# The end of an attention kernel: divisors through a permutation product, the residual in PSUM, projections moved into the last block, and a norm spread over more periods

## The chip, the cores and the metric

The kernel runs on one core of a Trainium2 chip. The time is the device time of one launch in microseconds (us), the median of several runs. Engines are named as the profile names them: PE is TensorE (matmul), DVE VectorE, ACT ScalarE, POOL GpSimd, and SP the queue that issues all DMAs here. Instructions of one engine start in the order in which the program lists them.

## What is computed

Two layers run on x of shape (2, 2048, 512) with a condition vector per batch row. The first is a state-space block: norm, a linear recurrence, a residual, and a feed-forward part. The second is attention with 16 heads of 32 features. Cut to what the change touches, the second layer ends so:

```python
energy = jnp.einsum('bhqd,bhkd->bhqk', q, k)
att = jax.nn.softmax(energy, axis=-1) / D ** 0.5
out = jnp.einsum('bhqk,bhkd->bhqd', att, v)
out = jnp.moveaxis(out, 1, 2).reshape(B, N, D)
out = out @ Wp.T + bp
h1 = out + hidden
h2 = _sln(h1, w, ln_g, ln_b, Wg, bg, Wb, bb)
return h2 + h1
```

`_sln` is a norm over the 512 features with a gain and a shift that come from the condition. `hidden` is the output of the first layer.

## The kernel before

**First layer, to about 1390 us.** Chunks of 512 rows pass through norm, recurrence and feed-forward; the norm is `ln_stats` with `rsqrt` (L116), four columns at a time: a first guess by integer arithmetic and three Newton steps of four VectorE instructions each. `rsqrt` is called 24 times here, and once at the very end of the kernel.

**Attention, from about 1450 us.** A block is one batch row, one pair of heads and 512 queries; there are 64, listed in `blocks`, and the last of batch 1 are ordered so that the queries 1536 to 2047 of the last two pairs come at the end. A block takes eight periods. In a period TensorE makes scores: two maxima probes `m` (`across`, L773), one or two score tiles that are kept (`keep`, L762), sometimes a score tile that is made again (`make`, L816), and the products of probabilities with values for two key tiles of the period before (`weighted`, L828). VectorE reads `m` (`top`, L785), keeps a running maximum (`run`, L771) and shifts the fresh scores (`pT`, L820); GpSimd shifts the kept ones (`take_off`, L812); ScalarE copies kept scores (L766) and takes exponentials (L825). Score tiles `s` have two PSUM buffers, `m` has one. The block runs ahead: maxima of a block are gathered 15 periods before they are used, and the shift of a block goes through DRAM and back into a tile of 128x1024 (`spread`, L799).

Values carry 32 columns of ones, so that the output `o` of a pair, one PSUM tile, holds the outputs of two heads in partitions 0 to 31 and 96 to 127 and their divisors, each repeated 32 times, in partitions 32 to 63 and 64 to 95. After the last key tile `weighted` copies `o` to `raw` (L842) and writes divisors to `sd` and outputs to `od` in DRAM.

**The order of everything else** is written out by hand. `after(j, what, ...)` puts work at the start of period j, `closing(j, what, ...)` after that period's second exponential. Entries of one period run in the order in which they were entered. In the text offset means the period within a block, 0 to 7.

When all heads of 512 queries are there, `fetch_sums`, `invert` (reciprocal, L875) and a write bring 1/divisor to `invd`. Each tile of 128 queries is then fetched (`fetch`, L878: six DMAs), divided on GpSimd (`divide`), projected (`project`: four matmuls), and normalised: `moments` (residual add, statistics), `deviation` (ten small VectorE instructions: 1/sqrt by three Newton steps), `last_norm` on ScalarE, and `add_t` and `close` on GpSimd, then the output DMA. For batch 0 the 16 tiles go beside the attention of batch 1, two tiles in each three blocks: projection in offsets 6, 7, 0 and 1, `moments` at the close of offset 1, `deviation` at the close of offset 2, `last_norm` and `add_t` in offset 5, `close` in offset 7. For batch 1 all steps of a tile are packed more densely.

**The last 512 queries of batch 1** have their own functions. `end_fetch` (L972) loads outputs, divisors and residual rows of the first twelve heads in one period before the last block, 19 DMAs; `end_fetch_more` loads the outputs of heads 12 and 13; `end_divide` divides on GpSimd. After the last block `end_project` (L1000) projects three groups of four heads, and `end_last` (L1010) sends the divisors of heads 12 to 15 through DRAM, inverts them, divides, projects the fourth group, adds the residual, and normalises and writes four tiles.

The lines that set the order of the end before:

```python
after(NP * (N - 1) + 3, end_fetch_more)
for g in range(NG - 1):
    after(j + 5 + g, end_divide, g)
after(NP * N + 2, end_project, list(range(NG - 1)))
after(NP * N + 20, end_last)
```

with j two periods ahead of the last block, whose first period is `NP * (N - 1)`.

Of the kernel before, what the change touches and what calls it, by code (L numbers as in the profile page):

```python
# [8 lines left out]
F32 = mybir.dt.float32  # L9
# [3 lines left out]
I32 = mybir.dt.int32  # L13
# [6 lines left out]
P = 128  # L20
# [19 lines left out]
def tile_s5_block_then_sln_attention(  # L40
# [75 lines left out]
    def rsqrt(v, y, n):  # L116

        nc.vector.tensor_scalar(
            y.bitcast(I32), v.bitcast(I32), -0.5, float(0x5F3759DF), ALU.mult, ALU.add
        )  # L120
        for _ in range(3):
            a = small.tile([P, n], F32, name="rs_a", tag=f"rs_a{n}")
            nc.vector.tensor_mul(a, y, y)
            b = small.tile([P, n], F32, name="rs_b", tag=f"rs_b{n}")
            nc.vector.tensor_mul(b, a, v)
            c = small.tile([P, n], F32, name="rs_c", tag=f"rs_c{n}")
            nc.vector.tensor_scalar(c, b, -0.5, 1.5, ALU.mult, ALU.add)
            nc.vector.tensor_mul(y, y, c)

    def ln_stats(src, n, mean, rstd):  # L130

# [696 lines left out]
    def weighted(n, kt, first, final):  # L828

        if first:  # L830
            outs[n] = ps_o.tile([P, CH], F32, name="o")
        x = probs.pop((n, kt))
        v = vst[pair_of[n] % 2]
        for e in range(2):
            nc.tensor.matmul(  # L835
                outs[n][64 * e : 64 * e + 64, :], v[:, kt, e : e + 2, :], x[:, e, :],
                start=first, stop=final,
            )
        if final:
            b, p, c = blocks[n]  # L840
            raw = work.tile([P, CH], F32, name="raw")
            nc.scalar.copy(raw, outs.pop(n))  # L842
            cols = slice(c * CH, (c + 1) * CH)
            for e in range(2):
                j = 2 * p + e
                nc.sync.dma_start(sd[b][j : j + 1, cols], raw[32 + 32 * e : 33 + 32 * e, :])
            for e in range(2):
                j = 2 * p + e
                if n == len(blocks) - 1:
                    dst = ends["o"][1][64 + HD * e : 64 + HD * e + HD, 1, :]  # L850
                else:
                    dst = od[b][HD * j : HD * j + HD, cols]
                nc.sync.dma_start(dst, raw[96 * e : 96 * e + 32, :])


    held, ending = {}, {}
# [51 lines left out]
            nc.tensor.matmul(py, o4[:, g, :], wp[:, g, :], start=g == 0, stop=g == NG - 1)  # L908
        held[b, qt] = o4, h, py

    def moments(b, qt):

        o4, h, py = held[b, qt]
        nc.vector.tensor_add(h, py, h)
        st = small.tile([P, 6], F32, name="st3")
        nc.vector.bn_stats(st, h)
        mv = small.tile([P, 2], F32, name="mv3", bufs=4)
        nc.vector.bn_aggr(mv, st)
        held[b, qt] = h, o4.rearrange("p g q -> p (g q)"), mv

    def add_t(b, qt):
        h, ht, *_ = held[b, qt]
        nc.gpsimd.tensor_tensor(ht, h, ending[b][1], ALU.add)

    def deviation(b, qt):

        h, ht, mv = held[b, qt]
        v = small.tile([P, 1], F32, name="v3")
        c = small.tile([P, 1], F32, name="c3")
        y = small.tile([P, 1], F32, name="scale3", bufs=3)  # L930
        shift = small.tile([P, 1], F32, name="shift3", bufs=3)
        nc.vector.tensor_scalar(v, mv[:, 1:2], EPS, None, ALU.add)
        nc.vector.tensor_scalar(
            y.bitcast(I32), v.bitcast(I32), -0.5, float(0x5F3759DF), ALU.mult, ALU.add
        )
        nc.vector.tensor_scalar(v, v, -0.5, None, ALU.mult)
        for _ in range(3):
            nc.vector.tensor_scalar(c, y, y, v, ALU.mult, ALU.mult)
            nc.vector.tensor_scalar(y, c, 1.5, y, ALU.add, ALU.mult)
        nc.vector.tensor_scalar(shift, mv[:, 0:1], -1.0, y, ALU.mult, ALU.mult)  # L940
        held[b, qt] = h, ht, y, shift

    def last_norm(b, qt):

# [19 lines left out]
        nc.sync.dma_start(out[b, qt * P : (qt + 1) * P, :], y)  # L964


    LB, LC = NB - 1, NQ - 1

    def spare(name):
# [2 lines left out]
    def end_fetch():  # L972
        cols = slice(LC * CH, (LC + 1) * CH)
        ends["o"] = [spare("o01"), spare("o23")]
        ends["by"] = [spare("by01"), spare("by23")]
        ends["h"] = [spare("h01"), spare("h23")]
        for g in range(NG - 1):
            nc.sync.dma_start(ends["o"][g // 2][:, g % 2, :], od[LB][g * P : g * P + P, cols])
            end_divisors(range(4 * g, 4 * g + 4))
        for t in range(TT):  # L980
            at = slice((LC * TT + t) * P, (LC * TT + t + 1) * P)
            nc.sync.dma_start(ends["h"][t // 2][:, t % 2, :], x2[LB][at, :])

    def end_fetch_more():
        cols = slice(LC * CH, (LC + 1) * CH)
# [7 lines left out]
                ends["by"][j // 8][at, j // 4 % 2, :], invd[LB][j : j + 1, cols].to_broadcast([HD, CH])  # L993
            )

    def end_divide(g):
        o, by = ends["o"][g // 2][:, g % 2, :], ends["by"][g // 2][:, g % 2, :]
        nc.gpsimd.tensor_tensor(o, o, by, ALU.mult)

    def end_project(groups):  # L1000
        if "py" not in ends:
            ends["py"] = [ps.tile([P, 2, CH], F32, name="py4", tag="s", bufs=2) for _ in range(2)]
        for t in range(TT):
            for g in groups:
                nc.tensor.matmul(
                    ends["py"][t // 2][:, t % 2, :], ends["o"][g // 2][:, g % 2, t * P : (t + 1) * P],
                    wp[:, g, :], start=g == 0, stop=g == NG - 1,
                )

    def end_last():  # L1010
        late = slice(NH - 4, NH)
        fetch_sums(LB, LC, late, 32)
        invert(LB, LC, late, 32)
        end_divisors(range(NH - 4, NH))
        o, by = ends["o"][1][:, 1, :], ends["by"][1][:, 1, :]
        nc.vector.tensor_tensor(o, o, by, ALU.mult)
        end_project([NG - 1])
        g_row, t_row = ending[LB]
        mv = small.tile([P, TT, 2], F32, name="mv4")
        for t in range(TT):  # L1020
            h, py = ends["h"][t // 2][:, t % 2, :], ends["py"][t // 2][:, t % 2, :]
            nc.vector.tensor_add(h, py, h)
            st = small.tile([P, 6], F32, name="st3")
            nc.vector.bn_stats(st, h)
            nc.vector.bn_aggr(mv[:, t, :], st)
        v = small.tile([P, TT], F32, name="v4")
        scale = small.tile([P, TT], F32, name="scale4")
        shift = small.tile([P, TT], F32, name="shift4")
        nc.vector.tensor_scalar(v, mv[:, :, 1], EPS, None, ALU.add)
        rsqrt(v, scale, TT)  # L1030
        nc.vector.scalar_tensor_tensor(shift, mv[:, :, 0], -1.0, scale, ALU.mult, ALU.mult)
        for t in range(TT):
            qt = LC * TT + t
            h = ends["h"][t // 2][:, t % 2, :]
            y = ends["o"][t // 2][:, t % 2, :]
            nc.scalar.activation(y, h, AF.Identity, bias=shift[:, t : t + 1], scale=scale[:, t : t + 1])
            nc.gpsimd.tensor_tensor(h, h, t_row, ALU.add)  # L1037
            nc.vector.tensor_tensor(y, y, g_row, ALU.mult)  # L1038
            nc.vector.tensor_tensor(y, y, h, ALU.add)  # L1039
            nc.sync.dma_start(out[LB, qt * P : (qt + 1) * P, :], y)  # L1040


# [44 lines left out]
    for b in range(NB):  # L1087
        for c in range(NQ):
            j = NP * (blocks.index((b, NPAIR - 1, c)) + 1) + 1
            if (b, c) == (LB, LC):  # L1090
                most = slice(0, NH - 4)
                j = NP * (N - 1) - 2
                after(j - 3, fetch_sums, b, c, most)
                after(j - 1, invert, b, c, most)
                after(j + 1, end_fetch)
                after(NP * (N - 1) + 3, end_fetch_more)
                for g in range(NG - 1):
                    after(j + 5 + g, end_divide, g)
                after(NP * N + 2, end_project, list(range(NG - 1)))
                after(NP * N + 20, end_last)  # L1100
                continue
            after(j, fetch_sums, b, c)
            after(j + 2, invert, b, c)
# [2 lines left out]
            for t in range(TT):  # L1106
                qt = c * TT + t
                if b == LB:
                    k = j + 3 + 2 * t
                    after(k + 3, project, b, qt)  # L1110
                    after(k + 3, moments, b, qt)
                else:

                    k = NP * (NPAIR * NQ * (b + 1) + 2 + 3 * qt // 2) + 3
                    for g in range(NG):
                        after(k + 3 + g, project, b, qt, (g,))
                    closing(k + 6, moments, b, qt)
                last = k + 3 if b == LB else k + 6
                after(k if b == LB else k - 2, fetch, b, qt)
                after(k + 2, divide, b, qt)  # L1120
                (after if b == LB else closing)(last + 1, deviation, b, qt)
                after(last + (2 if b == LB else 4), last_norm, b, qt)
                after(last + (3 if b == LB else 6), close, b, qt)
                if b != LB:
                    after(last + 4, add_t, b, qt)

    def run_due(j):
        for what, args in due.pop(j, ()):
# [117 lines left out]
```

## Time and profile before

| what | us |
|---|---|
| median of 3 runs | 3510.64 |
| lowest, highest | 3507.99, 3518.59 |
| the profiled execution | 3509.6 |
| its span in the profile | 3507.7 |

The profiled execution ran at a mean granted TensorE clock of 0.991. Busy time by stage, from the view that gives each engine's busy time in stretches (columns: stretch, length, then busy us of PE, its weight loads, DVE, ACT, POOL with the number of instructions, granted clock, DMA share, GB/s):

```profile
400.00:1300.00 900.00, 899.83 (x2316) 413.09 (x2315) 254.99 (x569) 136.04 (x197) 218.38 (x162) 1.00 0.12 42
...
1500.00:2000.00 500.00, 489.19 (x2093) 221.90 (x2093) 453.61 (x451) 444.10 (x484) 406.38 (x172) 1.00 0.28 67
...
2500.00:3000.00 500.00, 476.61 (x1941) 212.32 (x1941) 434.96 (x538) 403.57 (x440) 407.44 (x193) 1.00 0.33 79
...
3460.00:3508.00 48.00, 23.68 (x68) 8.07 (x68) 24.91 (x54) 9.74 (x12) 16.52 (x11) 0.83 0.12 42
```

In the first layer PE is busy all the time. In attention alone (1500 to 2000) PE has 97.8%, and VectorE, ScalarE and GpSimd have 81% to 91%. In the stretch in which batch 0 is normalised beside it (2500 to 3000) PE falls to 95.3%. In the last 48 us no engine is busy for more than half of the time.

### The profile page before, as it was taken

Reading aid. Unit: us, or ns where it says so; the run is one execution under the profiler, and the core shown is the slowest. Engines: PE = TensorE matmul, PEld = TensorE weight load, DVE = VectorE, ACT = ScalarE, POOL = GpSimd, SP = SyncE. Lnnn points to the kernel's source line nnn. Section 1 sums busy time; section 2 is a strip of 40 time slices with the busy share of each in tenths; the row PEclk is TensorE's granted clock in tenths of the full one; section 3 lists DMA queues with packets and bytes.
Section 4 is the critical chain, followed back from the end, with each engine's and each line's share of the span. In section 5 each row is a group of like instructions: output and inputs, shape, how many; then the busy total and the mean of one; then the engine's idle time right before and its main releaser. Section 6 shows DMA issues by size and latency. Waiting matters only on the chain. (4 is left out here: it accounts for less than half of the span.)

```text
span 3507.7 us, 34138 instructions
## 1 busy us (share of the span) xinstructions
PE 3362.0 (96%) x11752; PEld 1526.4 (44%) x11752; DVE 2229.1 (64%) x3136; ACT 1897.0 (54%) x2147; POOL 1997.6 (57%) x1020
## 2 busy tenths in 40 slices
PE   7999999999999999899999999999999999999986
PEld 4444444444444444444444444444444444444432
DVE  6233232323232311589999999999888888888885
ACT  2111112111111111388888888888878888887853
POOL 4223131313131311288888888888878887888885
PEclk8999999999999999999999999999999999999998
DMA  8001111111111112322223222323233333233233
GB/s 300 1 30 42 48 39 45 39 45 39 51 36 36 36 42 66 114 69 66 56 65 71 65 67 52 71 67 73 68 88 75 73 84 82 71 83 90 58 98 99
DMA packets 201709, 237.07 MB, mean 68 GB/s; under 512 B 89856, under 2 KB 119040, under 8 KB 197440
## 3 DMA queue, kind: packets, MB, share of 16 engines
q1 hardware_dynamic: 201536, 234.89, 24.4%
q8 instruction: 93, 1.52, 0.2%
q14 instruction: 80, 0.66, 0.1%
HBM read 166.91 MB, written 67.76 MB: 67 GB/s over the span
## 5 line engine op out<-in xcount | busy, mean ns | idle before, releaser
L814 POOL TENSOR_TENSOR x<-x,shift 128x1024 f32<-128x1024 f32 x640 | 1501.3, 2385 | 289.4 <-DMA shift<-flat 227.0
L766 ACT COPY x<-s 128x1024 f32<-128x1024 f32 x640 | 635.3, 1013 | 262.3 <-PE s L755 261.1
L755 PE MATMUL s<-qs,ks 128*128 128x512 f32 x2048 | 698.7, 431 | 39.8 <-DVE run L771 36.1
L825 ACT ACTIVATE x<-x 128x1024 f32<-128x1024 f32 x640 | 676.4, 1057 | 27.1 <-POOL x L814 27.1
L771 DVE TENSOR_TENSOR run<-s,run 128x1024 f32<-128x1024 f32 x512 | 625.1, 1221 | 64.6 <-ACT x L766 46.9
L835 PE MATMUL o<-x,v 128*64 128x512 f32 x2560 | 664.6, 614 | 0.8 <-ACT x L825 0.8
L785 DVE TENSOR_REDUCE top<-m 128x1 f32<-128x768 f32 x512 | 486.1, 949 | 25.1 <-PE m L780 24.7
L820 DVE TENSOR_TENSOR pT<-s,shift 128x1024 f32<-128x1024 f32 x384 | 467.7, 1218 | 52.7 <-PE s L755 47.1
L755 PEld LDWEIGHTS s<-qs,ks 128*128 128x128 f32 x2048 | 344.7, 189 | 299.0 <-DVE run L771 129.2
L502 PE MATMUL po<-w_sb,hid 128*128 128x512 f32 x1024 | 460.3, 592 | 0.0
L489 PE MATMUL ph<-fT,w_sb 128*128 128x512 f32 x1024 | 459.7, 593 | 0.0
L825 ACT ACTIVATE pT<-pT 128x1024 f32<-128x1024 f32 x384 | 407.3, 1061 | 63.0 <-DVE pT L820 50.3
L493 ACT ACTIVATE hid<-ph,vec 128x512 f32<-128x512 f32 x128 | 88.0, 687 | 591.4 <-PE ph L489 591.4
L835 PE MATMUL o<-pT,v 128*64 128x512 f32 x1536 | 395.1, 593 | 4.6 <-ACT pT L825 4.6
L160 DVE SCALAR_TENSOR_TENSOR lo<-pk,vec,hi 128x512 fp32r<-128x512 f32 x64 | 48.1, 751 | 502.5 <-ACT hi L159 496.9
L780 PE MATMUL m<-ks,qs 128*128 128x384 f32 x1024 | 284.8, 359 | 23.7 <-DVE top L785 22.1
L489 PEld LDWEIGHTS ph<-fT,w_sb 128*128 128x128 f32 x1024 | 191.9, 190 | 226.5 <-issue 226.5
L502 PEld LDWEIGHTS po<-w_sb,hid 128*128 128x128 f32 x1024 | 191.1, 190 | 221.5 <-issue 221.5
L436 POOL TENSOR_TENSOR m<-m,m 128x512 f32<-128x512 f32 x8 | 13.1, 1642 | 442.2 <-DVE m L434 442.2
L159 ACT ACTIVATE hi<-pk,vec 128x512 fp32r<-128x512 f32 x64 | 44.0, 687 | 393.0 <-PE pk L532 388.4
L835 PEld LDWEIGHTS o<-x,v 128*64 128x64 f32 x2560 | 138.6, 135 | 259.8 <-issue 147.8
L512 POOL TENSOR_TENSOR x<-x,gated 128x512 f32<-128x512 f32 x32 | 39.6, 1269 | 349.5 <-DVE gated L511 349.5
(241 smaller groups left out, 2831.7 us busy)
## 6 DMA issues: line engine op xcount, KB each, us to landing
ks<-kd SPq DMA_DIRECT2D x128, 256.0 KB
qs<-qd SPq DMA_DIRECT2D x512, 64.0 KB
shift<-flat SPq DMA_DIRECT2D x64, 512.0 KB
x<-in_x SPq DMA_DIRECT2D x8, 1024.0 KB
w_sb<-in_w SPq DMA_DIRECT2D x8, 1024.0 KB
x<-x SPq DMA_DIRECT2D x8, 1024.0 KB
kd<-hi SPq DMA_DIRECT2D x32, 256.0 KB
kd<-lo SPq DMA_DIRECT2D x32, 256.0 KB
```

The source lines that it names most:

```text
L489: nc.tensor.matmul(ph, w1_sb[:, k, f * P : (f + 1) * P], fts[b, c][:, k, :], start=k == 0, stop=k == KC - 1)
L493: nc.scalar.activation(hids[f], ph, AF.Gelu_apprx_tanh, bias=vec[:, V_B1 + f : V_B1 + f + 1], scale=1.0)
L502: nc.tensor.matmul(pos[b, c][:, t, :], hid[:, t * P : (t + 1) * P], w2_sb[:, f, :], start=f == 0, stop=f == FC - 1,)
L755: nc.tensor.matmul(s[:, e, :], kst[pair_of[n], e][:, kt * P : (kt + 1) * P], qst[n][:, e, :], start=True, stop=True,)
L766: nc.scalar.copy(x, s)
L771: nc.vector.tensor_tensor(runs[n], s, kept[n, 0] if kt == 1 else runs[n], ALU.max)
L780: nc.tensor.matmul(m[:, i, :YW], qst[n][:, e, t * P : (t + 1) * P], kst[pair_of[n], e][:, k : k + YW], start=True, stop=True,)
L785: nc.vector.tensor_reduce(tops[n][:, j, 0:1], m[:, :, :YW], AX.XY, ALU.max, negate=True)
L814: nc.gpsimd.tensor_tensor(x, x, shifts[n], ALU.add)
L820: nc.vector.tensor_tensor(x, s, shifts[n], ALU.add)
L825: nc.scalar.activation(x, x, AF.Exp)
L835: nc.tensor.matmul(outs[n][64 * e : 64 * e + 64, :], v[:, kt, e : e + 2, :], x[:, e, :], start=first, stop=final,)
```

## The change

1. `rsqrt` makes a Newton step of three instructions instead of four (two `scalar_tensor_tensor`).
2. For the tiles of batch 0, `moments` becomes `residual` and `statistics`, and `deviation` can be run in two parts: the guess and one step, then two steps and the shift. Their places move: residual at the close of offset 1, statistics of offset 2, the parts of offsets 4 and 5; `add_t` in offset 6, `last_norm` in offset 7, `close` in offset 0 of the next block. The tiles of batch 1 keep their periods.
3. The end. The residual rows are put into PSUM by a product with the identity (`end_begin`), and projections are added to it. Two of the four tiles are begun and projected in periods 6 and 7 of the last block, the other two in the period of the last weighted product, ahead of it; there the fourth group is projected too, with the outputs of heads 12 and 13 and zeros in its other half. Heads 12 and 13 get their divisors through DRAM during the last block.
4. The last pair of heads is no longer sent through DRAM. `end_last` copies `o` by halves and multiplies it by a permuted identity, `turn`, that brings each head's divisors to the partitions of its outputs; VectorE takes the reciprocal and the product; a weight tile `w`, which is zero but for the rows of these two heads, projects the result onto the sum. Statistics are read from PSUM. ScalarE copies each sum and GpSimd adds the shift row to the copy; the last add is on VectorE for even tiles and on GpSimd for odd ones.
5. `end_fetch` also clears and fills `w` and `turn`: two memsets and three copies on GpSimd, two DMAs. `end_fetch_more` comes two periods earlier.

The diff, cut:

```diff
-            nc.vector.tensor_mul(b, a, v)
-            c = small.tile([P, n], F32, name="rs_c", tag=f"rs_c{n}")
-            nc.vector.tensor_scalar(c, b, -0.5, 1.5, ALU.mult, ALU.add)
-            nc.vector.tensor_mul(y, y, c)
+            nc.vector.scalar_tensor_tensor(b, a, -0.5, v, ALU.mult, ALU.mult)
+            nc.vector.scalar_tensor_tensor(y, b, 1.5, y, ALU.add, ALU.mult)
...
-        if final:
+        if final and n == len(blocks) - 1:
+            end_last(outs.pop(n))
+        elif final:
...
+        late = P - 2 * HD
+        nc.gpsimd.memset(ends["o"][1][late:, 1, :], 0.0)
+        nc.gpsimd.memset(ends["w"], 0.0)
+        nc.gpsimd.tensor_copy(ends["turn"], ident)
+        for e in range(2):
+            to, of = 3 * HD * e, HD + HD * e
+            nc.sync.dma_start(ends["w"][to : to + HD, :], wp[late + HD * e : late + HD * e + HD, NG - 1, :])
+            nc.gpsimd.tensor_copy(ends["turn"][:, to : to + HD], ident[:, of : of + HD])
...
+    def end_begin(i):
+        if i:
+            ends["py", i] = ps.tile([P, 2, CH], F32, name="py4", tag="s", bufs=2)
+        else:
+            ends["py", i] = ps.tile([P, 2, CH], F32, name="py3", tag="m")
+        for t in range(2):
+            nc.tensor.matmul(ends["py", i][:, t, :], ident, ends["h"][i][:, t, :], start=True, stop=False)
...
+    def end_last(o):
+        raw, inv, on = (spare(n)[:, 0, :] for n in ("raw4", "inv4", "on4"))
+        turned = ps.tile([P, 2, 2 * P], F32, name="turned", tag="pt")
+        for i in range(2):
+            at = slice(2 * i * P, 2 * (i + 1) * P)
+            nc.scalar.copy(raw[:, at], o[:, at])
+            nc.tensor.matmul(turned[:, i, :], ends["turn"], raw[:, at], start=True, stop=True)
+        for i in range(2):
+            at = slice(2 * i * P, 2 * (i + 1) * P)
+            nc.vector.reciprocal(inv[:, at], turned[:, i, :])
+            nc.vector.tensor_tensor(on[:, at], o[:, at], inv[:, at], ALU.mult)
...
         for t in range(TT):
+            py = ends["py", t // 2][:, t % 2, :]
+            nc.tensor.matmul(py, on[:, t * P : (t + 1) * P], ends["w"], start=False, stop=True)
             st = small.tile([P, 6], F32, name="st3")
-            nc.vector.bn_stats(st, h)
+            nc.vector.bn_stats(st, py)
             nc.vector.bn_aggr(mv[:, t, :], st)
+            ht = hts[t // 2][:, t % 2, :]
+            nc.scalar.copy(ht, py)
+            nc.gpsimd.tensor_tensor(ht, ht, t_row, ALU.add)
...
-            nc.vector.tensor_tensor(y, y, h, ALU.add)
+            (nc.gpsimd if t % 2 else nc.vector).tensor_tensor(y, y, ht, ALU.add)
...
+                j = NP * (N - 1)
+                after(j - 5, fetch_sums, b, c, most)
+                after(j - 3, invert, b, c, most)
+                after(j - 1, end_fetch)
+                after(j + 1, end_fetch_more)
+                after(j + 1, fetch_sums, b, c, rest, 32)
+                after(j + 4, invert, b, c, rest, 32)
+                after(j + 5, end_divisors, range(NH - 4, NH - 2))
                 for g in range(NG - 1):
-                    after(j + 5 + g, end_divide, g)
-                after(NP * N + 2, end_project, list(range(NG - 1)))
-                after(NP * N + 20, end_last)
+                    after(j + 3 + g, end_divide, g)
+                after(j + 8, end_divide, NG - 1, P // 2)
+                after(j + 6, end_begin, 0)
+                for g in range(NG - 1):
+                    after(j + 6 + g // 2, end_project, 0, [g])
+                after(j + 8, end_begin, 1)
+                after(j + 8, end_project, 1, list(range(NG - 1)))
+                for i in range(2):
+                    closing(j + 8, end_project, i, [NG - 1])
...
-                    closing(k + 6, moments, b, qt)
+                    closing(k + 6, residual, b, qt)
+                    closing(k + 7, statistics, b, qt)
+                    closing(k + 9, deviation, b, qt, (0,))
+                    closing(k + 10, deviation, b, qt, (1,))
+                    after(k + 11, add_t, b, qt)
+                    after(k + 12, last_norm, b, qt)
+                    after(k + 13, close, b, qt)
```

## The prediction

> **What bounds the kernel now.** I read the page first, then who waited for whom on TensorE in two stretches of the attention, then the timeline of one normalised tile, then the timeline of the end.
>
> ```profile
> span 3507.7 us, 34138 instructions
> PE 3362.0 (96%) x11752; PEld 1526.4 (44%) x11752; DVE 2229.1 (64%) x3136; ACT 1897.0 (54%) x2147; POOL 1997.6 (57%) x1020
> ```
>
> TensorE is busy nearly everywhere, so an edit counts where TensorE waits, or where it has nothing left to do: the end. The next lines are TensorE's waits: the first from 1600 to 2400 us, where attention runs alone, the other two from 2500 to 3300 us, where the finished tiles of batch 0 are normalised beside it (columns: total us, times, longest).
>
> ```profile
> PE s L755 <- DVE run L771: 14.0, 57, 0.3
> ...
> PE m L780 <- DVE top L785: 18.8, 16, 1.2
> PE s L755 <- DVE run L771: 14.7, 42, 2.4
> ```
>
> The middle line is new in the second stretch: 16 times, once per tile, near 1.18 us each. Its cause in the timeline of one tile:
>
> ```profile
> 2803.26 0.15 DVE L932 TENSOR_SCALAR v<-mv 128x1 f32<-128x1 f32 x1
> ...
> 2805.49 0.21 DVE L940 TENSOR_SCALAR shift<-mv,scale 128x1 f32<-128x1 f32 x1
> 2805.62 1.22 DVE L820 TENSOR_TENSOR pT<-s,shift 128x1024 f32<-128x1024 f32 x1
> ...
> 2807.76 0.62 PE L780 MATMUL m<-ks,qs 128*128 128x384 f32 x2 [1.18 <-DVE top L785]
> ```
>
> Ten small instructions hold VectorE for 2.36 us, and its three large ones of the next period come late. Starts of L780 give the length of each period. Without a tile, from offset 0 on: 4.02, 4.25, 3.35, 3.20, 4.00, 3.87, 3.34, 2.78, sum 28.8. With one: +0.85, +0.86, +0.56, +1.04 where its four projections sit (offsets 6, 7, 0, 1), then -0.35, 0, +1.50, +0.50: 4.96 per tile, of which 3.31 is TensorE's own work and 1.65 the norm's.
>
> The end (start, duration, engine, line):
>
> ```profile
> 3455.81 3.70 PE L908 MATMUL py<-wp,o 128*128 128x512 f32 x8 [1.51 <-POOL o L895]
> ...
> 3461.77 0.73 PE L755 MATMUL s<-qs,ks 128*128 128x512 f32 x2
> ...
> 3466.99 1.08 PE L835 MATMUL o<-pT,v 128*64 128x512 f32 x4 [0.75 <-ACT pT L825]
> 3468.91 1.08 PE L835 MATMUL o<-x,v 128*64 128x512 f32 x4 [0.84 <-ACT x L825]
> 3470.72 1.08 PE L835 MATMUL o<-pT,v 128*64 128x512 f32 x4 [0.73 <-ACT pT L825]
> 3471.73 10.57 PE L1005 MATMUL py<-wp,o 128*128 128x512 f32 x24
> 3471.85 0.59 ACT L842 COPY raw<-o 128x512 f32<-128x512 f32 x1 [1.18 <-PE o L835]
> 3476.35 0.34 DVE L875 RECIPROCAL sm<-sm 64x32 f32<-64x32 f32 x1 [6.83 <-DMA sm<-sd]
> 3482.11 0.69 DVE L1016 TENSOR_TENSOR o<-o,by 128x512 f32<-128x512 f32 x1 [5.42 <-DMA by<-invd]
> 3484.88 0.69 DVE L1022 TENSOR_TENSOR h<-py,h 128x512 f32<-128x512 f32 x1 [2.08 <-PE py L1005]
> 3494.16 2.93 ACT L1036 ACTIVATE o<-h,shift,scale 128x512 f32<-128x512 f32 x4 [21.73 <-DVE shift L1031]
> 3496.86 1.73 DVE L1039 TENSOR_TENSOR o<-o,h 128x512 f32<-128x512 f32 x1 [1.16 <-POOL h L1037]
> ```
>
> From the last copy at 3471.85 to the end at 3507.73 are 35.9 us: 10.3 of DMA round trip for four heads' divisors, with 12 projections (24 records) beside it, 2.8 to the first sum, 9.3 of moments and rsqrt, 13.5 of output.
>
> **What the Trainium skill says.** "PSUM — Partial Sum Buffer", Engine vs sequencer instructions: matmuls start and complete in program order; in this trace no later matmul passes a waiting one, so what is put ahead of the last weighted product delays it. "VectorE: DVE Perf Modes", First, the fixed hardware budget: reciprocal is an iterative divide with a repeat count of 8. The trace has 0.544 us for 128x64 and 0.165 for 128x1, so 6.0 ns a column (5.8 cycles at the page's 0.96 GHz); I take the trace. "GPSIMD Engine Reference", 1. Specifications: its SBUF interfaces are shared with VectorE and contend with instructions that read two SBUF inputs; the trace agrees (L1039 1.73 us beside GpSimd, 0.69 alone at 3504.03).
>
> **The norm of batch 0's 16 tiles.** It is the same work: residual 0.71 in offset 1, statistics 0.83 in offset 2, then halves of about 1.1 and 1.2 in offsets 4 and 5. Before, residual and statistics lay in offset 1, where VectorE has only two large operations (some 2 us spare), and the 2.36 in offset 2. So 0.83 leaves a free place. Following one tile by its starts: the stall at m in offset 3-4 goes (1.50 becomes about 0.1), offset 4-5 keeps 0.3. Then it depends on the next tile. Of each three blocks two end with projections. There VectorE waits for TensorE by 1.06, 0.98 and 0.87 us (starts 2783.39, 2787.60, 2791.69), which swallows the halves but for 0.3: the tile costs -0.35+0.1+0.3+0.3 = about 0.3, not 1.65. In the other eight tiles no projection follows, VectorE is idle only 0.21 and 0.14 us in those periods, and of its 3.1 us of added work in offsets 2 to 5 about 2.4 reach TensorE: -0.35+2.4 = 2.1. Sum: 8 x (1.65-0.3) - 8 x (2.1-1.65) = 7.2 gained. GpSimd's closing pair (2 x 1.28) moves from offset 7, where it waits for shift anyway, to offset 0 between take-offs: 2.8 to 7 us of lead normally cover it; in the two of four late blocks (load of new keys) that hold a closing I charge 0.6 each. **-6.0.** Bounds: +7 if all tiles are of the second kind (and none of it gained elsewhere), -26.4 if nothing of the 1.65 is left.
>
> **The shorter rsqrt.** Three of 15 small instructions less, 0.2 each. Two of 24 calls lie ahead of idle TensorE (5.51 us wait at 74.41, 0.42 at 25.92), the others beside a full TensorE: **-1.2**, bounds -2.5 and 0; 0.6 more in the end below.
>
> **The last block.** Added on TensorE ahead of the last weighted product: 4 products with the identity, 12 projections, and 4 of the half-filled last group: 20 of 0.86 us (two records 0.43 apart) = 17.2, and two breaks of 0.3 before scores. All start after 3461.77, and from there TensorE has 7.3 us of its own against 10.1 measured: 2.75 idle to fill. The last copy comes 15.0 later. SyncE: two more row copies (0.45 each) at the end of the long fetch push the fetch of the third tile, for whose divide GpSimd waits 4.4 us at 3442.5: 1.0 more, on the path. GpSimd's two memsets (0.53 by L1147) and three small copies, about 2 us, lie ahead of that wait and vanish in it. The earlier fetches wait for od and sd to land, some 2 us, in front of the fourth tile's fetch; GpSimd comes to its divide at 3454.49, fetches issued by 3445.8, so I charge nothing; it costs up to 3 if landing takes longer. Divisors of heads 12 and 13 have 10 us to spare. **+16.0** in all.
>
> **The end.** Zero is the start of the first half's copy. Copies 0.38 each (between 0.24 for 128 columns and 0.59 for 512); the turn of half 2 ends near 1.5; reciprocals of 256 columns 1.7 each, products 0.36; the second product ends at 5.7. The first projection runs beside this. VectorE at 3484.88 started only when both tiles of one py buffer were written, though it needs one; so I expect the second tile's product to wait for the first one's readers: statistics of the four tiles start at 5.7, 7.6, 8.5, 10.4. The first activation was 3.26 after the last aggregate and becomes 2.66: 13.8. Output: two multiplies and an add, GpSimd adds for odd tiles, contention for about 1.5: last instruction ends near 21.3; the DMA tail was 3.0. End at 24.3, not 35.9: **-11.6** (the 10.3 round trip and four residual adds go, 3.4 of reciprocals and two waits on buffers come). Bounds -14.5 without these waits, -9 with slower PSUM reads.
>
> Sum on the profiled execution (3507.7 span plus 1.9 around it = 3509.6): -6.0-1.2+16.0-11.6 = -2.8, so 3506.8. The median is 1.0 above that execution: about 3508.
>
> **Rivals.** (1) The halves are swallowed in both kinds of tile: -26.4 in place of -6.0, total -23.2, 3487. For it: the 1.18 waits are exactly 16. Against: VectorE has 0.35 us idle where no projection follows. (2) Slower: GpSimd's moved closing delays the take-offs of the new block. It decides when shift lands less than 7.05 us (three take-offs of 2.35) plus the closing's 2.56 before the second period's exponential. Leads there are 1.2 to 2 us: 8 x 1.36 + 8 x 0.56 = +15.4, total +12.6, 3523. For it: GpSimd waits 227 us for shift over the kernel; against: VectorE's lag makes the block late anyway. (3) The change doesn't delay the last product as said, as ScalarE or GpSimd hold the block longer and TensorE has more room: 9 less, 3499. Against: program order.
>
> **How the numbers follow.** Chances: forecast 0.53, (1) 0.17, (2) 0.25, (3) 0.05. About 0.3% (10.5 us) can be told from no change. The forecast's own range is 3498 to 3517 and lies within it but for a tenth on each side; with (1) and part of (3) faster has 0.25; of (2) a third stays within: same 0.54, slower 0.21. Eight in ten: from the middle of (1), 3488, to beyond (2), 3526.
>
> **What would show it.** The wait of m for top gone or below 8 us from 2500 to 3300; periods at offsets 5 to 0 longer in every third block; the last copy of o near 3481, and some 24 us from it to the end; 20 more matmuls before it. Wrong if tiles of both kinds cost the same, if take-offs are what ScalarE waits for at a block's start, or if the last weighted product starts before 3476.

## The result and the profile after

| | us |
|---|---|
| median after, 20 runs | 3518.73 (3512.81 to 3525.17) |
| median before, 20 runs beside them | 3511.43 (3505.02 to 3518.59) |
| ratio, with its 95% interval | 1.0020 [1.0013, 1.0027] |
| profiled execution after, its span | 3512.81, 3511.0 |

The change makes the kernel 7 us slower, and the interval leaves no doubt of the direction. The forecast was 2 to 3 us less. The first lines of the page after:

```profile
span 3511.0 us, 34088 instructions
PE 3374.7 (96%) x11772; PEld 1528.8 (44%) x11772; DVE 2210.4 (63%) x3058; ACT 1900.5 (54%) x2152; POOL 2005.7 (57%) x1028
```

TensorE has 12.7 us more and the span is only 3.3 us longer, although the medians lie 7.3 apart: the profiled execution after is the fastest of its 20. That gap is taken up below, under the clock.

TensorE's waits from 2500 to 3300 us, as shown of before (total us, times, longest):

```profile
PE s L753 <- DVE run L769: 22.8, 47, 2.1
PE s L753 <- DVE v L931: 3.9, 16, 0.3
```

The 18.8 us of `m` for `top` are gone, as forecast. But the wait for `run` has grown from 14.7, and a new one of 0.3 per tile stands behind the first part of `deviation`: 12 of the 18.8 have come back under other names.

The timeline of the end after (start, duration, engine, line):

```profile
3481.64 0.65 ACT L1043 COPY raw<-o 128x256 f32<-128x256 f32 x2 [11.87 <-PE o L833]
...
3483.23 1.76 DVE L1047 RECIPROCAL inv<-turned 128x256 f32<-128x256 f32 x1 [14.61 <-PE turned L1044]
...
3487.92 0.69 DVE L1056 BATCH_NORM_STATS2 st<-py 128x6 f32<-128x512 f32 x1
3488.64 0.58 ACT L1059 COPY ht<-py 128x512 f32<-128x512 f32 x1 [6.36 <-DVE st L1056]
...
3489.28 3.78 PE L1054 MATMUL py<-w,on 128*128 128x512 f32 x4 [2.22 <-ACT ht L1059]
...
3491.39 0.70 DVE L1056 BATCH_NORM_STATS2 st<-py 128x6 f32<-128x512 f32 x1 [2.57 <-PE py L1054]
...
3496.59 0.70 DVE L1056 BATCH_NORM_STATS2 st<-py 128x6 f32<-128x512 f32 x1 [2.57 <-PE py L1054]
...
3498.14 1.12 DVE L125 SCALAR_TENSOR_TENSOR rs_b<-rs_a,v 128x4 f32<-128x4 f32 x1
...
3500.87 2.78 ACT L1070 ACTIVATE h<-py,shift,scale 128x512 f32<-128x512 f32 x4 [2.96 <-DVE shift L1066]
```

The last copy of `o` begins at 3481.64 (forecast: near 3481). From there the end takes 29.4 us, not 24.3. The reader should follow one tile: product, statistics, copy, and only then the product of the second tile of the pair, which waits for the copy (2.22). The four statistics start 6.3, 9.8, 11.5 and 15.0 us after the copy; forecast were 5.7, 7.6, 8.5 and 10.4.

Where the profiled execution's 3.3 us come from, by the starts of the copy of `o` at the end of each block: start-up and first layer +0.1, blocks 34 to 62 -5.2, the last block +14.9, the end -6.5.

### The profile page after: what moved, and what is told of

Read it like the earlier page. It is cut to its first block, busy times and chain, and to the rows that moved or that the text cites. A ratio compares the mean times of both kernels' runs of the same rounds, so it can differ in the third digit from the quotient of the medians.

```text
span 3511.0 us, 34088 instructions
## 1 busy us (share of the span) xinstructions
PE 3374.7 (96%) x11772; PEld 1528.8 (44%) x11772; DVE 2210.4 (63%) x3058; ACT 1900.5 (54%) x2152; POOL 2005.7 (57%) x1028
```

## The experiments

All times below are medians; ratios are against runs of the kernel before on the same chip, with their 95% intervals. A ratio isn't exactly the quotient of two medians (`nr_pick`: 0.9977, by the medians 0.9981).

| kernel | what it is | us | ratio |
|---|---|---|---|
| r_only | before + shorter rsqrt | 3512.92 | 0.9998 [0.9989, 1.0006] |
| n_only | before + spread norm | 3510.99 | 0.9999 [0.9991, 1.0007] |
| e_only | before + last block and end | 3520.73 | 1.0025 [1.0016, 1.0034] |
| nr | rsqrt and norm, end of before | 3510.43 | 0.9994 [0.9986, 1.0002] |
| sep | change, four products first | 3517.49 | 1.0013 [1.0007, 1.0020] |
| late_sep | sep, ten products behind the turn | 3514.17 | 1.0001 [0.9993, 1.0009] |
| n_even | before + norm spread for even tiles | 3512.09 | 0.9992 [0.9984, 1.0000] |
| n_close | n_only, closing pair at offset 7 | 3518.53 | 1.0016 [1.0009, 1.0023] |
| n_even_close | n_even, closing pair at offset 7 | 3510.59 | 0.9993 [0.9984, 1.0001] |
| late_sep_even | late_sep with the norm of n_even | 3511.55 | 0.9998 [0.9990, 1.0006] |
| nr_even_close | rsqrt + n_even_close, end of before | 3509.29 | 0.9992 [0.9984, 1.0001] |
| late_even_close | late_sep with the norm of n_even_close | 3513.18 | 1.0000 [0.9992, 1.0008] |
| nr_pick | rsqrt + norm spread for five tiles, end of before | 3505.93 | 0.9977 [0.9968, 0.9986] |
| late_pick | the same with the end of late_sep, one add moved | 3508.89 | 0.9985 [0.9979, 0.9992] |

The median of before lay between 3512.4 and 3513.8 in these comparisons.

### The parts alone

`r_only`, `n_only` and `e_only` each take one part of the diff: the lines of `rsqrt`; those of `residual`, `statistics`, `deviation` and the places of batch 0's tiles; those of `end_*` and the last block. `nr` takes the first two.

> The kernel before with the shorter rsqrt alone. My theory: it gains. In the profile of the whole change the first feed-forward product after the start-up came 1.36 us earlier, so 1.4 to 3 us less than before, unless TensorE's clock falls to half once more in the start-up. The rival (the shorter rsqrt only moves the moments at which TensorE idles, and the clock gate takes back more than it gives): equal or up to 3 us slower.

> The kernel before with the norm of batch 0 spread alone. My theory: the per-block times of the two profiles fell by 5.2 us between blocks 34 and 62; 1.7 of that lay in one block where the kernel before had one 3.4 us stretch at half clock, which needn't be there in every run. So 3.5 to 5.2 us faster than before. Rival (the spread work leaves more short idle stretches on TensorE, and its clock falls more often): no gain, or slower by up to 3.

> The kernel before with the last block and the end changed alone. My theory: the last block costs 14.9 and the end gives back 6.5, so 8.4 us slower than before. Rival (the typical run of the whole change is 4 us slower than its profiled one, and this lies in the end): 12 or more slower. With the two other parts alone the three differences must add up to about +7.3, the difference of the medians, if the parts don't touch one another.

> The whole change without its last block and end: the kernel before with the shorter rsqrt and the spread norm. My theory (the parts add up; what makes the change slower is the last block and the end alone): the norm gives 3.2 us in a profile with as many stretches at half clock as the other, the rsqrt 1.05, so 4 us faster than before and 11 to 12 us faster than the whole change. Rival (the norm's gain is eaten by more stretches at half clock): equal to before within 1.5 us.

The end alone costs what the block times said, 0.25%, and what the whole change costs; `nr` gains 0.06%, an interval that reaches zero. So the end is the part that loses, and the parts add up: 1.0025 times 0.9994 is 1.0019. The two others can't be told from no change when they stand alone, and my figure for the norm, taken from one pair of profiles, was too high.

**The shorter rsqrt** is found in the start-up. The first wait for the norm ends at 73.05 us after, 74.41 before: 1.36 us earlier. Then (start, duration; the kernel before first, the kernel after second, the same eight products):

```profile
97.16 3.68 PE L489 MATMUL ph<-fT,w_sb 128*128 128x512 f32 x8
```

```profile
97.00 5.97 PE L487 MATMUL ph<-fT,w_sb 128*128 128x512 f32 x8
```

TensorE's granted clock was at half from 94.8 to 101.6 us in the profile after and took back more than the gain. The shorter rsqrt has a part in it. Here is a window of 3.41 us ahead of this place, before first, then after (stretch, length, busy us of PE, its loads, DVE, ACT, POOL, granted clock, DMA share, GB/s; what windows are follows under the clock):

```profile
92.00:95.41 3.41, 2.65 (x24) 1.13 (x16) 0.00 (x0) 0.59 (x1) 0.00 (x0) 1.00 0.00 0
```

```profile
91.40:94.81 3.41, 2.35 (x20) 1.12 (x16) 0.00 (x0) 0.76 (x2) 0.00 (x0) 1.00 0.00 0
```

All ten profiles with the shorter rsqrt have such a stretch, starting at 94.6 to 97.9 us, behind a window with 2.06 to 2.44 us of TensorE's work. Of the six with the old rsqrt only two have it (`n_only` and `n_even_close`, behind 2.05 and 2.51 us); in the other four no window there has less than 2.62. That fits the rival put down for `r_only`: the earlier start moves TensorE's work against the windows, and the clock takes the gain back. The first copy of `o` comes at 1514.8 us on average in the ten profiles and at 1514.6 in the six. Only at equal clock is the gain seen: two profiles with the same half-clock stretches in the first layer, `n_only` without and `sep` with the shorter rsqrt, reach that copy at 1517.58 and 1516.53 us: 1.05 gained, 1.2 forecast.

**The clock.** The Trainium skill, "TensorE: Matmul & The Clock Gate", Part 1, What's actually happening, says that TensorE runs at half clock until it has been busy, and again after an idle window, judged in windows of 3413 ns that don't start with the kernel. The traces agree on the length: stretches at half clock last 3.4 us or a multiple. But the window ahead of one need not be idle. The view of engines by stretch, of the kernel before (stretch, length, busy us of PE, its loads, DVE, ACT, POOL, granted clock, DMA share, GB/s):

```profile
2597.40:2600.80 3.40, 1.01 (x5) 0.67 (x4) 2.05 (x2) 3.40 (x5) 3.40 (x2) 1.00 0.00 0
2600.80:2604.20 3.40, 3.26 (x10) 1.06 (x10) 3.37 (x5) 2.86 (x4) 3.40 (x3) 0.50 0.27 68
```

A window with 1.01 us of work, in a block whose shift came late, is followed by one at half clock. Between 1520 and 3425 us the sixteen profiles have 34 such stretches. Each comes right behind a window with at most 1.81 us of work, and no window with less than 1.46 goes without; between the two some are followed by half clock and some are not. In the start-up windows with up to 2.51 us were followed by it (above), so busy time alone doesn't give the limit. One stretch costs up to 1.6 us: block 50 took 33.48 us with one and 31.84 without (`sep` and the change). It can also cost nothing: in `n_even` block 57 took 32.40 with one, the like block 54 32.35 without. Where the windows fall differs from run to run, and so does the number of stretches: none in the change's profile, one in that of before, 0 to 3 and 2.1 on average in all. The change's profile was the lucky one. Laying windows at every phase over its trace, with 1.6 us of work as the limit, gives one to three stretches, 1.8 on average (1.0 with 1.46 as the limit, 3.1 with 1.81). At 1.6 us each that is an estimate of some 3 us, half of the 5.9 us between that execution and the median of its runs; that the gap comes from there is argued and not shown. The rest is open. The mean granted clock was 0.989 in that execution and 0.986 to 0.988 in the four that took longest, but three runs at 0.990 took 3517.6 to 3519.0 us, so the clock alone doesn't put the runs in order.

### The end

`sep`, in `end_last`:

```diff
+        for t in range(TT):
+            py = ends["py", t // 2][:, t % 2, :]
+            nc.tensor.matmul(py, on[:, t * P : (t + 1) * P], ends["w"], start=False, stop=True)
         mv = small.tile([P, TT, 2], F32, name="mv4")
...
         for t in range(TT):
             py = ends["py", t // 2][:, t % 2, :]
-            nc.tensor.matmul(py, on[:, t * P : (t + 1) * P], ends["w"], start=False, stop=True)
             st = small.tile([P, 6], F32, name="st3")
```

> The whole change, with the four last products on TensorE put ahead of all statistics and copies, so that no product waits for the readers of the product before it in the same PSUM tile. My theory: these waits are the 4.6 us by which the statistics of the last tile came later than forecast; the last statistics then come 4 to 5 us earlier (near 10 to 11 us after the first half's copy, not 14.95), and the whole is 4 to 5 us faster than the whole change. Rival (TensorE at half clock after its wait, and VectorE's own work, set the pace): the products stay 0.85 us a record apart and at most 1.5 us is gained.

Its end (same view):

```profile
3491.53 0.65 ACT L1043 COPY raw<-o 128x256 f32<-128x256 f32 x2 [11.87 <-PE o L833]
...
3495.82 4.11 PE L1051 MATMUL py<-w,on 128*128 128x512 f32 x8 [2.73 <-DVE on L1048]
...
3501.34 0.70 DVE L1058 BATCH_NORM_STATS2 st<-py 128x6 f32<-128x512 f32 x1 [0.43 <-ACT ht L1061]
...
3502.29 0.80 DVE L1066 TENSOR_SCALAR v<-mv 128x4 f32<-128x4 f32 x1
3503.13 1.18 DVE L118 TENSOR_SCALAR scale<-v 128x4 int32<-128x4 int32 x1
...
3506.31 2.78 ACT L1072 ACTIVATE h<-py,shift,scale 128x512 f32<-128x512 f32 x4 [3.66 <-DVE shift L1068]
```

The last statistics start 9.8 us after the copy, not 15.0: the lost 4.6 us are back, and a little more. But two things went at once, the waits for readers and the half clock that came with them. The eight records of the products now take 4.11 us, at full clock; in the change the middle four alone took 3.78, 0.85 us apart: TensorE had 1.12 us of work in the window up to 3487.7 us and stood at half clock from there to the end. There the way to the last statistics leads through three products (of the second, third and fourth tile). An estimate from these lines: each is slower by 0.85 us (two records 0.85 apart, not 0.43), so that some 2.5 of the 5.1 us are the half clock, and the rest are the waits themselves. Then 0.7 us goes again: two `tensor_scalar` take 0.80 and 1.18 us in place of 0.17, because GpSimd's adds, until then spread between the statistics, now run beside the rsqrt. From copy to end it is 24.9 us. So the waits were the cause, as my theory had it, and the rival's bound of 1.5 us is wrong; but the half clock that the rival named is part of what the waits cost. The ratios show some 2.5 us of it (1.0013 for 1.0020), and their intervals overlap, so the timing alone would not have settled it.

`late_sep` does this and also moves the second pair's ten products:

```diff
             nc.tensor.matmul(turned[:, i, :], ends["turn"], raw[:, at], start=True, stop=True)
+        end_begin(1)
+        end_project(1, list(range(NG)))
...
-                after(j + 8, end_begin, 1)
-                after(j + 8, end_project, 1, list(range(NG - 1)))
-                for i in range(2):
-                    closing(j + 8, end_project, i, [NG - 1])
+                closing(j + 8, end_project, 0, [NG - 1])
```

> The whole change, with the four last products ahead of all statistics, and the ten products of the second pair of tiles (two with the identity, eight projections) moved from in front of the last weighted product to behind the turn. My theory: the last copy comes 8.6 us earlier than with the four products alone moved; of the ten products 2.75 us lie in TensorE's wait for the divided x and the rest delays the last statistics from 9.8 to about 13.7 us after the copy. So 4 to 5 us faster than with the four products alone moved, 8 to 9 faster than the whole change, and no slower than before. Rival (TensorE does the same work in another place, and nothing but the place changes): no faster than with the four products alone moved.

The last block takes 49.2 us in place of 56.9, and the last statistics start 15.4 us after the copy. It is level with before and 0.19% better than the change (6.7 us; 8 to 9 were expected). The missing part: the statistics of the four tiles and the copies of the same PSUM tiles still take turns, 3.5 us from the first to the last, where I had reckoned with the products alone.

### The norm of batch 0

`n_even` keeps the spread norm for even tiles alone; the odd ones have their places of before:

```diff
                     closing(k + 6, residual, b, qt)
+                    if qt % 2:
+                        closing(k + 6, statistics, b, qt)
+                        closing(k + 7, deviation, b, qt)
+                        after(k + 10, last_norm, b, qt)
+                        after(k + 12, close, b, qt)
+                        after(k + 10, add_t, b, qt)
+                        continue
```

> The kernel before with the norm spread only for the eight even tiles of batch 0, behind which the next tile's projections lie; the odd ones keep their steps of before. My theory (each tile's gain or loss is its own): the five blocks 35, 38, 44, 47 and 50 each 1.2 to 1.6 us shorter, the blocks 42, 54 and 57 back at 30.85 us and not 32.54, 36, 39, 45, 48 and 51 back at 31.2; 8 to 9 us less from block 33 to block 58 than before, when the half-clock stretches are as many. Rival (the 1.7 us in blocks 42, 54 and 57 come from the block ahead of each being served earlier, whatever the odd tile does): these three stay near 32.5, and the gain is 4 us at most.

`n_close` and `n_even_close` put GpSimd's closing pair back ahead of the new block:

```diff
-                    after(k + 11, add_t, b, qt)
-                    after(k + 12, last_norm, b, qt)
-                    after(k + 13, close, b, qt)
+                    after(k + 10, add_t, b, qt)
+                    after(k + 11, last_norm, b, qt)
+                    after(k + 12, close, b, qt)
```

> The kernel before with the norm spread for all sixteen tiles of batch 0, but GpSimd's closing pair back at offset 7 (the normalised tile one period earlier for it), ahead of the next block's take-offs. My theory now: in the blocks whose shift comes late, GpSimd has a backlog of ten take-offs, and the closing pair of 2.56 us that the change put between the second and the third of them delays the rest; that is the 1.5 to 1.7 us of blocks 42, 54 and 57. So these come back to about 31 us, and blocks 33 to 58 take 4 to 5 us less than with the spread norm alone, some 8 less than before. Rival (VectorE's added work in these blocks does it): they stay at 32.5.

> The same, spread for the even tiles alone. My theory: blocks 42, 54 and 57 at 30.85, 36, 39, 45, 48 and 51 at 31.2, the five even ones 1.2 to 1.6 shorter: 9 us less than before from block 33 to 58 with as many half-clock stretches, 0.2 to 0.3% faster than before. Rival as above: 4.5 us, as with the even tiles alone.

Times from copy of `o` to copy of `o`, us, worked out from the traces (a star: half clock in part of the block):

```
block                  before  n_only  n_even  n_close  n_even_close
35 (44, 47 alike)       33.77   32.20   32.21   33.03    33.03
36 (39, 45, 48, 51)     31.20   31.34   31.20   32.16    31.21
42                      30.85   32.54   32.30*  31.82    30.85
54                      30.87   32.54   32.35   31.82    32.32*
57                      30.85   32.54   32.40*  31.82    30.84
```

Without half clock these blocks repeat to within 0.1 us from profile to profile of kernels that treat them alike, so that a few tenths can be read where the whole time can't tell 3 us. Blocks whose shift comes late (late blocks; the others are punctual) don't repeat so well: block 41 took from 34.2 to 36.4 us. Blocks 42, 54 and 57 each follow a late block that has an even tile to close. They stay slow in `n_even`, against my theory and as the rival had it, and come back in `n_even_close`. The odd tile keeps its old places in both, so it is the even tile's: its closing pair moved, and with it `add_t` and `last_norm` by one period. The timeline names the pair. GpSimd around the start of block 42, first with the closing of before (`r_only`), then with that of the change (`nr`):

```profile
2717.07 1.27 POOL L961 TENSOR_TENSOR y<-y,o 128x512 f32<-128x512 f32 x1
2726.55 18.75 POOL L812 TENSOR_TENSOR x<-x,shift 128x1024 f32<-128x1024 f32 x8 [8.20 <-DMA shift<-flat]
```

```profile
2723.65 4.70 POOL L812 TENSOR_TENSOR x<-x,shift 128x1024 f32<-128x1024 f32 x2 [9.21 <-DMA shift<-flat]
2728.31 1.27 POOL L972 TENSOR_TENSOR y<-y,g_row 128x512 f32<-128x512 f32 x1
2729.66 1.28 POOL L973 TENSOR_TENSOR y<-y,o 128x512 f32<-128x512 f32 x1
2730.89 16.44 POOL L812 TENSOR_TENSOR x<-x,shift 128x1024 f32<-128x1024 f32 x7
```

Before, the pair ran in the 8 us in which GpSimd waited for the late shift. After, it waits until the shift has come and then pushes seven take-offs back by 2.6 us. But offset 7 is worse for the rest. `n_close`, from which I expected 8 us less than before, is slower than before: 0.8 us more than `n_only` in each punctual block with a tile. The same holds for `n_even_close`: blocks 35, 44 and 47 gain 0.74 us each and not 1.2 to 1.6, and blocks 33 to 58 take 808.7 us, with two half-clock stretches (one of double length) where before has 809.0 with one; 9 us less were expected at as many stretches. At offset 7 `last_norm` comes too late for GpSimd, which stands with the take-offs of the new block behind it (GpSimd's waits from 2500 to 3300 us in `n_close`, then in before):

```profile
POOL y L974 <- ACT y L964: 78.7, 16, 6.0
```

```profile
POOL y L962 <- ACT y L952: 26.1, 8, 4.8
```

### Put together

> The whole change with both: second pair's ten products behind the turn and the four last products ahead of the statistics, and the norm spread for the even tiles alone. If the parts add up, it is faster than before by 4 to 8 us and the fastest of all; if the odd tiles' share is not what costs, it equals the kernel with the first two edits alone.

> The shorter rsqrt and the norm spread for the even tiles with the closing pair in its old place, and the last block and the end of before. If the parts add up: 9 to 10 us faster than before (0.27%), faster than both kernels. If the norm's gain is made up of half-clock stretches that come and go: no more than 3 us.

> The same norm and rsqrt with the change's end, the second pair's ten products behind the turn and the four last products ahead of the statistics. If the parts add up, 4 to 5 us faster than the same kernel with the closing pair at offset 0, so 5 to 7 us faster than before, and 2 to 4 slower than the same norm and rsqrt with the end of before. If the new end is worth something at last: faster than that one.

All three fall short of what was expected, and none can be told from before by its interval. The two with the new end don't differ as expected, and `nr_even_close` has less than the 9 us hoped for, since offset 7 takes half of what each early tile gains.

`nr_pick` draws the conclusion: the spread norm with the closing pair at offset 0 for the five tiles to which both apply, with projections behind them and no late block ahead of them:

```diff
-                    if qt % 2:
+                    if qt not in (0, 2, 6, 8, 10):
```

> The shorter rsqrt, the norm spread (closing pair at offset 0) for the five tiles alone whose period groups hold projections and whose next block's shift is not late (tiles 0, 2, 6, 8, 10), everything else, the end too, as before. My theory (the closing pair's place is what a late block pays for, and in other blocks it is free at offset 0): blocks 35, 38, 44, 47 and 50 each 1.57 us shorter (1.2 with a half-clock stretch), 42, 54 and 57 at 30.85, the second kind at 31.2, so 7.5 us less from block 33 to 58 at as many half-clock stretches as before, and 0.2% to 0.25% faster than before. Rival (the profile's gain is spent again elsewhere): no more than the 0.08% of the even tiles.

> The same norm and rsqrt, with the change's end in its best form: the second pair's ten products behind the turn, the four last products ahead of the statistics, and VectorE adding the last tile's row itself behind the shift, so that GpSimd holds VectorE up by one add less in the rsqrt. My theory: the first activation comes 3.0 us after the last aggregate and not 4.06, and the whole is 1 us better in the end than with ten products behind the turn, 5 to 7 us faster than before, and within 2 us of the kernel with the end of before. Rival (the new end costs more than before's in any form): 3 us or more slower than that one.

`nr_pick` is 0.23% faster than before, 0.43% faster than the change by the two ratios, and its blocks are those expected: 35, 44 and 47 at 32.2, 42, 54 and 57 at 30.85, 36 at 31.2. From block 33 to 58 it takes 803.1 us with two half-clock stretches, where before takes 809.0 with one. `late_pick` differs from it in the last block and the end alone (three GpSimd adds, the fourth on VectorE behind the shift). The first activation now comes 3.06 us after the last aggregate, not 4.06 as in `late_sep`:

```profile
3496.93 2.78 ACT L1076 ACTIVATE h<-py,shift,scale 128x512 f32<-128x512 f32 x4 [2.65 <-DVE shift L1071]
```

It beats before as well, but is 3.0 us slower than `nr_pick` by the medians: its last block takes 8.7 us more and its end 5.8 less. That is at the rival's bound of 3 and outside the 2 of my theory; the two intervals overlap, so it rests on the traces and on three such pairs that agree. `nr` and `late_sep`, `nr_even_close` and `late_even_close`, `nr_pick` and `late_pick` differ in the last block and the end, and each time the new end is slower by 0.07% or 0.08%. In no form that was tried does it pay.

## Why the prediction was wrong, point by point

- **The last block, +16.0:** measured 14.9 (15.7 in `e_only`). Twenty products of 0.86 us ahead of the last weighted one are 17.2 us. They fill TensorE's idle time there (2.3 us by the trace of before, forecast 2.75; none is left after) and delay the rest by what remains, 14.9 us.
- **The end, -11.6:** measured -6.5. This is the step that failed; alone it turns the forecast sum of -2.8 into +2.3. The prediction had seen that a second tile's product waits for the first one's readers, but its 1.9 us from one statistics of a pair to the next left no room for ScalarE's copy and took full clock for granted. The copy waits for the statistics of the same PSUM tile (it starts 0.03 us after they end) and the next product for the copy, and TensorE has by then fallen to half clock: 3.5 us instead of 1.9. By the estimate above 0.85 of these 1.6 us are the half clock, the rest is near the copy's 0.58. `sep` takes the wait away and has the statistics at 9.8 in place of 15.0. One more us is the 1.12 us `scalar_tensor_tensor` in the rsqrt beside a GpSimd add. The output part and the 3.0 us behind the last instruction were right: 10.2 us from the first activation, 10.5 forecast.
- **The norm, -6.0:** the profile after has -5.3 from block 33 to 58, which looks like a hit. Of this some 1.6 is the half-clock stretch that before's profile had and this one lacked. Counting 1.6 for each stretch, five profiles with the change's norm have 803.9 us on average (803.1 to 805.5) and three without it 806.9 (805.2 to 808.2): an estimate of -3.0. The kind of step was right: five tiles of the first kind (even ones, with projections behind them) gain up to 1.57 each (forecast 1.35), five of the second kind lose 0.15 (forecast 0.45). The mis-sized term is the closing pair in late blocks: charged 0.6 in two blocks, it costs 1.5 in three, and the tiles of the first kind in 41, 53 and 56 gain too little to be told from the scatter of these blocks, which wait for the shift anyway. That is rival 2's mechanism, but not its place and price: it was to cost 0.56 to 1.36 in all sixteen blocks, and it costs 1.5 in three with a late shift and nothing in the punctual ones.
- **rsqrt, -1.2:** -1.05 at equal clock. Before the first copy of `o` nothing of it is left, since all ten profiles with the shorter rsqrt have one more half-clock stretch near 95 us and four of the six without it don't. The prediction had no term for the clock.
- **From the profile to the median, +1.0:** the sum was made against one execution of before. The change's own profiled execution lay 5.9 below its median. The corrected terms give -3.0, -1.05, +14.9 and -6.5, so +4.4, or +5.4 if the clock takes the rsqrt's gain, against +7.3 by the medians, where the ratio's interval reaches from 4.6 to 9.5 us. What lies between is not settled.
- **Luck and rivals:** the median of 3518.7 lies nearer to rival 2's 3523 than to the forecast's 3508, but not for rival 2's reason: `e_only`, without the moved closing pair, has the whole loss. Rival 1 is out (a norm of -3.0, not -26.4), and so is rival 3 (the last copy was delayed as said).
- **What would show it:** the wait of `m` gone, the last copy near 3481 and the periods longer in each third block came as said. The 24 us from the last copy did not come.

## What to carry to other kernels

When a chain of small steps moves into the place of a round trip through DRAM, count every reader of each PSUM tile, since the next write of the tile waited here for the last of them, and ask what TensorE's clock does during the wait; putting all writes ahead of all reads brought the last statistics 5.1 us closer. Twelve projections beside the round trip of before cost next to nothing (10.6 us of products in 10.3 us of waiting); twenty products ahead of the last weighted product cost 14.9 us. And before work is moved on an in-order engine, look at what it is moved behind: GpSimd's closing pair was free in the wait for a late shift and cost 1.5 us behind it, while in punctual blocks the opposite place was the better one, so that no single place suited all tiles.

## What the runs showed of the hardware

- TensorE fell to half clock for 3.4 us after windows with up to 1.81 us of work in the attention and up to 2.51 us in the start-up, not only after idle ones, and the places differ from profile to profile. So an edit that makes work end earlier may cost a stretch: all ten profiles with the shorter rsqrt have one that four of six without it lack. One profiled execution lay 5.9 us from the median of its kernel; the times of blocks whose shift isn't late repeat to within 0.1 us and are the better measure.
- Beside a GpSimd add of 128x512 a `tensor_scalar` of 128x4 on VectorE took up to 1.18 us in place of 0.17. The Trainium skill, "GPSIMD Engine Reference", 1. Specifications, says that GpSimd's SBUF interfaces contend with VectorE's instructions of two SBUF inputs or in a two-port mode; the trace agrees for instructions with two SBUF inputs (`scalar_tensor_tensor` of 128x4, 1.12 us in place of 0.16). `tensor_scalar` has one tensor input, and no run shows whether it ran in a two-port mode. The price looks like the rest of the running add (1.26 us each), however small VectorE's instruction is: in `sep` each of the two `tensor_scalar` ends 0.03 us after an add, and in `late_pick`, with one add less, the second takes 0.17 us again.
